# Layer 1 of a two-layer attention kernel: the output projection of a pair of rows as seven block products, with sums and residual on GpSimd

## Chip, cores and metric

The kernel runs on one core of a Trainium2 chip. The metric is the device time of one execution in microseconds, as the median of several runs. In the profile PE is the TensorE matrix engine, PEld its weight load, DVE VectorE, ACT ScalarE, POOL GpSimd and SP SyncE, which here only issues transfers.

## The reference, cut to what matters

The input x is 128 rows of 256 positions with 256 channels. Layer 0 (row attention with 8 heads and a bias from a second tensor) adds its output to x; nothing of it is touched here. Layer 1 normalizes x by groups, runs banded attention with 4 heads along the positions of each row, projects, and adds the result to x:

```python
qkv = x2 @ w_in.T + b_in                      # x2: 128 rows, 256 positions, 256 channels
q, k, v = split into 4 heads of 64
scores = q @ k.T / sqrt(64), kept where |i - j| <= 16
out = softmax(scores) @ v                     # back to 256 positions x 256 channels
y = out @ w_out.T + b_out
x = x + y
```

## The kernel before

Everything is float32. The output projection of one row is a 256x256 by 256x256 product; two rows are handled together, as a "pair", so layer 1 has 64 pairs. Its work is written in one hand-ordered loop (a manual schedule): each engine runs its instructions strictly in the order in which the Python calls issue them. An iteration p of the loop handles five pairs at different stages: `was` (pair p-1, whose second row is still to be applied and whose projection is due), `now` (p), `nxt` (p+1, whose q, k and v are being projected), `nn` (p+2, being centred) and `n3` (p+3, being loaded).

The steps that matter, by method:

- `scores(r)`: 32 small score matmuls of row r, an exp on ACT, and the band mask as a product with `bw` on POOL (L2020).
- `apply(r)`: the weighted values into the PSUM tiles `o_eo` (L2034), and the softmax sums into `su_eo` (L2042). `copy_sums`, `copy_odd` (ACT) and `join_sums`, `join_odd` (DVE) add the even and odd halves; `invert` is a reciprocal of 1.7 us on DVE (L2065), `weigh` the product of both on DVE (L2070), which gives `oT[r]`, the transposed attention output of the row. `weigh(1)` also issues a small store on SP.
- `product(n, i)` and `join(n, i)`: q, k and v (n = 0, 1, 2) of both rows of a pair as seven block products each, in Winograd's form of Strassen's scheme: 256x256 by 256x256 over a 2x2 grid, the two rows as one grid direction and the two halves of the channels as the other. Products accumulate in two PSUM banks x and y; ACT copies x out after products 1, 6 and 7, and after 4 to its place; DVE adds y and a copy after products 2, 5 and 3. For q and k a product is one matmul of 256 columns (L1956), for v two of 128 (L1952). The sums of weight blocks are made once (`mix_weights`), those of the input blocks by `differences` on POOL (L1918 to L1921).
- `turn` transposes the loaded pair on DVE (L1900), `centre(k)` normalizes one channel half on ACT (L1905), `add_bias` adds the output bias to the residual tile `xt` on POOL (L1911).
- `out_block(r, b)`: half the output projection of a row: two matmuls of 256 columns that accumulate over the two channel halves (L2088). They write `su_y[:, :, 1]`, half of a PSUM tile of two banks whose other half `su_y[:, :, 0]` holds the softmax sums (`su_eo`): bank 0 has `su_eo[0]` and the first block, bank 1 `su_eo[1]` and the second. `out_row` is two blocks and `keep_row`; `keep_row(r)` adds the residual on DVE (L2096), and after row 1 issues the store of the pair on SP.
- `some_checks(n)` pops small reductions and thresholds from a queue; they guard the fast path's assumptions. They are used up after some 28 pairs and come again in the last eight.

The order within an iteration before: scores of both rows; apply(1) of `was`; the products 1, 2, 6, 5, 7 of q and k with the joins of sums; join_odd, weigh and out_row(0) of `was`; products 4 and 3 of q and k; value products 1 and 2; apply(0) of `now`; then the value products 6, 5, 7, 4, 3 with the two out_blocks of row 1 among them, and at the end invert, weigh, the second centre, differences, add_bias and turn.

Of the kernel before, what the change touches and what calls it, by code (L numbers as in the profile page):

```python
# [16 lines left out]
P = 128  # L17
# [756 lines left out]
def fast_kernel(  # L774
# [134 lines left out]
    def rows(ap, s0, n):  # L909
        return ap[s0 : s0 + n].rearrange("s (b p) c -> p (s b) c", p=P)  # L910
# [333 lines left out]
    class Pair:  # L1244
# [251 lines left out]
        def keep_row(self, r):  # L1496
            s = 2 * self.p + r
            nc.vector.tensor_tensor(
                xo[:, (s % GB) * NB : (s % GB + 1) * NB, :], self.ps_y.rearrange("p (b c) -> p b c", b=NB),
                self.xt[:, r * NB : (r + 1) * NB, :], ALU.add,  # L1500
            )
            if (s + 1) % GB == 0:
                j = s // GB
                nc.sync.dma_start(
                    x1[j].rearrange("s (p b) c -> p s (b c)", b=NB), xo.rearrange("p (s b) c -> p s (b c)", b=NB)
                )
            n = GB if s < S - GB else GB // 2 if s < S - GB // 2 else GB // 4
            if (s + 1) % n == 0:
                at = s + 1 - n
                moments_of(xo[:, at % GB * NB : (at % GB + n) * NB, :], at, n)  # L1510
# [310 lines left out]
    with tc.tile_pool(name="l1", bufs=2) as sb, tc.tile_pool(  # L1821
# [10 lines left out]
        dev = lrs[0][:, :G]  # L1832
        each = head.rearrange("p n d -> p (n d)").rearrange("p (n c) -> p n c", n=2)
        wst = sb.tile([P, 4, 3, P], F32, name="wst", bufs=1)

        def norm1():

# [20 lines left out]
        def mix_weights():  # L1858

            a = [[w_in[:, k].rearrange("p (n m c) -> p m n c", n=3, m=KC)[:, m] for k in range(KC)]  # L1860
                 for m in range(KC)]
            s1, s2, s3, s4 = (wst[:, n] for n in range(4))
            nc.gpsimd.tensor_tensor(s1, a[1][0], a[1][1], ALU.add)
            nc.gpsimd.tensor_tensor(s2, s1, a[0][0], ALU.subtract)
            nc.gpsimd.tensor_tensor(s3, a[0][0], a[1][0], ALU.subtract)
            nc.gpsimd.tensor_tensor(s4, a[0][1], s2, ALU.subtract)
# [9 lines left out]
        class Pair1:  # L1876
# [55 lines left out]
            def product(self, n, i):  # L1932

                if len(self.ps) == n:
                    self.ps.append([mm1("ps_qk", n % 2) for _ in range(2)])
                    self.u.append(sm.tile([P, 3, I], F32, name="u1", tag=f"u{n}", bufs=2))
                x, y = (ps[:, :I] for ps in self.ps[n])
                w = lambda m, k: w_in[:, k, n * C + m * P : n * C + (m + 1) * P]
                b = lambda k, r: self.xgT[:, k, r * I : (r + 1) * I]
                to, lhs, rhs, start = {  # L1940
                    1: (x, w(0, 0), b(0, 0), True),
                    2: (y, w(0, 1), b(1, 0), True),
                    6: (x, wst[:, 1, n], self.dT[:, 1], False),
                    5: (y, wst[:, 0, n], self.dT[:, 0], True),
                    7: (x, wst[:, 2, n], self.dT[:, 2], False),
                    4: (x, w(1, 1), self.dT[:, 3], False),
                    3: (y, wst[:, 3, n], b(1, 1), False),
                }[i]
                if n == 2:
                    for b in range(NB):  # L1950
                        at = slice(b * P, (b + 1) * P)
                        nc.tensor.matmul(  # L1952
                            to[:, at], rhs[:, at], lhs, start=start and b == 0, stop=True, skip_group_check=True
                        )
                else:
                    nc.tensor.matmul(to, lhs, rhs, start=start, stop=True, skip_group_check=True)  # L1956
                u = self.u[n]
                if i in (2, 5, 3):
                    return
                at = (1, 6, 7, 4).index(i)  # L1960
                to = self.to[n](1, 0) if i == 4 else u[:, at]
                if n == 2:
                    nc.scalar.copy(to, x.rearrange("p (b c) -> p b c", b=NB) if i == 4 else x)
                else:
                    nc.scalar.activation(to, x, AF.Identity, bias=bin_c[:, n * KC + (at > 1) : n * KC + (at > 1) + 1])  # L1965
# [116 lines left out]
            def out_block(self, r, b):  # L2082
# [4 lines left out]
                for k in range(KC):  # L2087
# [2 lines left out]
                        start=(k == 0), stop=(k == KC - 1),  # L2090
                    )

            def keep_row(self, r):
                if r == 0:
                    self.yo = sb.tile([P, 2 * NB, C], F32, name="yo", tag="yo")
                nc.vector.tensor_tensor(  # L2096
                    self.yo[:, r * NB : (r + 1) * NB, :], self.y,
                    self.xt[:, r * NB : (r + 1) * NB, :], ALU.add,
                )
                s0 = 2 * self.p  # L2100
                if self.p == NP - 1:
                    nc.sync.dma_start(rows(out, s0 + r, 1), self.yo[:, r * NB : (r + 1) * NB, :])
                elif r == 1:
                    nc.sync.dma_start(rows(out, s0, 2), self.yo)
# [28 lines left out]
        def some_checks(n):  # L2133
            for _ in range(n):
                queue = late or checks
                if queue:
                    queue.pop(0)()
# [6 lines left out]
        with tc.manual_schedule():  # L2144
# [16 lines left out]
            look_all(eb.rearrange("p h b i -> p (h b i)"), math.exp(-20.0))  # L2161
            n_eb = cols[0]

            was = Nobody()
            for p in range(NP - 1):
                nn = pair1(p + 2) if p == 0 else n3
                n3 = pair1(p + 3)
                if p == 0:
                    nn.turn()
                if p == 1:  # L2170
                    mask_t = sb.tile([S, I], F32, name="mask_all", bufs=1)
                    nc.sync.dma_start(mask_t, mask)
                    look_all(mask_t, 1e-15)
                    n_mask = cols[0]
                    load_sums(rsum.rearrange("n q r c i -> (n q r c i)"), "sums0")
                if p == NP - LATE + 2:
                    load_sums(rsum1[: NP - LATE].rearrange("n q r i -> (n q r i)"), "sums1")

                now.scores(0)
                now.scores(1)  # L2180
                was.apply(1)
                nxt.begin_fast()
                was.copy_sums(1)
                nxt.product(0, 1)
                was.copy_odd(1)
                nxt.product(1, 1)
                was.join_sums(1)
                for n in range(2):
                    nxt.product(n, 2)
                    nxt.join(n, 2)  # L2190
                was.invert(1)
                some_checks(p > 0)
                for i in (6, 5, 7):
                    for n in range(2):
                        nxt.product(n, i)
                for n in range(2):
                    nxt.join(n, 5)
                was.join_odd(1)
                was.weigh(1)
                was.out_row(0)  # L2200
                for n in range(2):
                    nxt.product(n, 4)
                    nxt.product(n, 3)
                    nxt.join(n, 3)
                fast = p < NP - 2
                if fast:
                    nxt.product(2, 1)
                    nxt.product(2, 2)
                    nxt.join(2, 2)
                nn.centre(0)  # L2210
                some_checks(2 if p > NP - LATE else 0)

                now.apply(0)
                now.copy_sums(0)
                if fast:
                    nxt.product(2, 6)
                    nxt.product(2, 5)
                now.copy_odd(0)
                now.join_sums(0)
                was.out_block(1, 0)  # L2220
                if fast:
                    nxt.product(2, 7)
                now.join_odd(0)
                some_checks(2 if p > NP - LATE else p > 0)
                was.out_block(1, 1)
                if fast:
                    nxt.join(2, 5)
                was.keep_row(1)
                if fast:
                    nxt.product(2, 4)  # L2230
                    nxt.product(2, 3)
                    nxt.join(2, 3)
                now.invert(0)
                now.weigh(0)
                nn.centre(1)
                nn.differences()
                nn.add_bias()
                n3.turn()
                if p == NP // 2:
                    below(0, n_eb, math.exp(20.0))  # L2240
                    below(n_eb, n_mask, 1e15)
                was, now, nxt = now, nxt, nn

            now.scores(0)
            was.apply(1)
            was.copy_sums(1)
            was.copy_odd(1)
# [102 lines left out]
```

## Time and profile before

| | us |
|---|---|
| median of 3 runs | 3133.21 (3131.51 to 3134.19) |
| the profiled execution's own time | 3134.36 |
| its span in the profile | 3132.6 |
| one pair in layer 1 (2511.42 to 2528.80) | 17.38 |
| mean granted TensorE clock | 0.985 |

The span is the time from the first instruction of the program to the last; the execution's own time includes what lies around it. Layer 1 takes about the last third of the span. A row of the timeline gives the start, the length, engine, line, operation, output and inputs, shape and count of a run of equal instructions, and in brackets the idle time before it and what ended it. A row of a group by form gives busy time and mean nanoseconds of one, then the idle time of the engine before them.

### The profile page before, as it was taken

To read this page: it belongs to the slowest core of one execution; us is meant where nothing else is said; L and a number is where in the kernel's file an instruction comes from. 1 tells how busy PE (TensorE), PEld (TensorE's weight loads), DVE (VectorE), ACT (ScalarE), POOL (GpSimd) and SP (SyncE) were. 2 spreads that over 40 slices of the span, in tenths; PEclk is the share of its full clock that TensorE was granted. 3 is DMA by queue.
4 is the path that set the end of the run, shared out by engine and by line. 5 is a ranking of instruction groups with operands and counts; after the bars stand their busy time and mean duration, and the time that the engine had idled before them with its cause. 6 is when DMAs were issued, how large, how long until landed. Compare 5 with 4: busy or idle time off the path is not lost.

```text
span 3132.6 us, 80584 instructions
## 1 busy us (share of the span) xinstructions
PE 3017.0 (96%) x33630; PEld 2096.3 (67%) x33630; DVE 2398.1 (77%) x4007; ACT 1574.6 (50%) x2639; POOL 2271.3 (73%) x1635
## 2 busy tenths in 40 slices
PE   5589999999999999999999999899999999999998
PEld 3345555655555565555555655588888888888886
DVE  7986777777777777777777777588888877777788
ACT  3454444444444444444444444355555555555554
POOL 3469998988899889889998987455555555555553
PEclk9799999999999999999999999899999999999999
DMA  9952333323333332333333232544343444343431
GB/s 360 389 173 59 97 71 99 93 66 91 99 99 69 99 97 65 89 98 99 69 99 99 64 92 71 117 93 94 92 95 92 95 92 94 90 97 88 98 93 53
DMA packets 690951, 328.16 MB, mean 105 GB/s; under 512 B 538673, under 2 KB 639921, under 8 KB 689425
## 3 DMA queue, kind: packets, MB, share of 16 engines
q1 hardware_dynamic: 686176, 320.28, 39.9%
q8 instruction: 266, 4.36, 0.6%
q10 hardware_dynamic: 4400, 2.63, 0.3%
q14 instruction: 109, 0.88, 0.1%
HBM read 254.09 MB, written 68.75 MB: 103 GB/s over the span
## 4 chain that ended last, share of the span: by engine, by line
PE 90%; DMA 4%; DVE 3%; issue 1%; POOL 1%; ACT 1%; SPq 0%; POOLq 0%; ACTq 0%; DVEq 0%
PE ps_p L1364 22%; PE ps_qk L1956 12%; PE ps_sc L1401 9%; PE ps_ov L1436 7%; PE ps_su_y L2088 7%; PE ps_v L1382 7%; PE ps_qk L1952 7%; PE ps_y L1491 7%; PE ps_o L2034 4%; PE ps_su L1444 3%; PE ps_sc L2009 3%; PE ps_su_y L2042 2%; DMA xa<-in_x_dram 1%; DVE st L1199 1%; DMA zt<-in_z_dram 1%
## 5 line engine op out<-in xcount | busy, mean ns | idle before, releaser
L1425 POOL TENSOR_TENSOR eboth<-e 128x512 f32<-128x512 f32 x512 | 746.9, 1479 | 175.9 <-PE ps_su L1444 95.5
L1421 DVE TENSOR_TENSOR e<-ps_sc,eb 128x1024 f32<-128x1024 f32 x384 | 458.2, 1221 | 290.5 <-ACT ps_sc L1413 289.9
L1413 ACT ACTIVATE ps_sc<-ps_sc 128x1024 f32<-128x1024 f32 x384 | 375.4, 1007 | 439.4 <-PE ps_sc L1401 308.0
L1401 PE MATMUL ps_sc<-qT,kT 32*128 32x256 f32 x4096 | 296.1, 401 | 0.1
L1919 POOL TENSOR_TENSOR dT<-xgT,dT 128x256 f32<-128x256 f32 x63 | 46.1, 731 | 315.7 <-ACT xgT L1905 315.7
L2020 POOL TENSOR_TENSOR e<-e,bw 128x384 f32<-128x384 f32 x256 | 248.4, 1001 | 10.7 <-ACT e L2018 10.7
L1401 PEld LDWEIGHTS ps_sc<-qT,kT 32*128 32x128 f32 x4096 | 186.3, 184 | 103.6 <-issue 90.6
L2088 PE MATMUL ps_su_y<-w_out,oT 128*128 128x256 f32 x1008 | 254.5, 385 | 0.9 <-DVE sums L2059 0.9
L1491 PEld LDWEIGHTS ps_y<-wo,oT 128*128 128x128 f32 x1024 | 194.7, 190 | 83.9 <-issue 44.7
L1364 PE MATMUL ps_p<-xgT,wg 128*128 128x512 f32 x512 | 249.1, 609 | 1.6 <-ACT xgT L1333 1.6
L1364 PE MATMUL ps_p<-xnT,wq 128*128 128x512 f32 x512 | 247.5, 605 | 1.5 <-POOL xnT L1351 1.4
L1436 PE MATMUL ps_ov<-e,v 128*32 128x256 f32 x4096 | 248.2, 383 | 0.0
L1491 PE MATMUL ps_y<-wo,oT 128*128 128x256 f32 x1024 | 243.1, 381 | 3.5 <-POOL oT L1481 2.7
L1382 PE MATMUL ps_v<-wv,xnT 128*128 128x256 f32 x1024 | 242.2, 379 | 0.0
L1364 PE MATMUL ps_p<-xnT,wk 128*128 128x512 f32 x512 | 240.7, 592 | 0.0
L1382 PEld LDWEIGHTS ps_v<-wv,xnT 128*128 128x128 f32 x1024 | 194.9, 190 | 54.7 <-issue 31.5
L2065 DVE RECIPROCAL rv<-sums 128x256 f32<-128x256 f32 x128 | 223.1, 1743 | 0.0
L1965 ACT ACTIVATE u<-ps_qk,bin_c 128x256 f32<-128x256 f32 x378 | 174.7, 477 | 94.9 <-PE ps_qk L1956 94.9
L2088 PEld LDWEIGHTS ps_su_y<-w_out,oT 128*128 128x128 f32 x1008 | 181.8, 190 | 22.4 <-DVE sums L2059 1.3
L1436 PEld LDWEIGHTS ps_ov<-e,v 128*32 128x32 f32 x4096 | 120.2, 110 | 109.2 <-issue 42.5
L1364 PEld LDWEIGHTS ps_p<-xnT,wk 128*128 128x128 f32 x512 | 97.2, 190 | 122.8 <-issue 122.8
L1371 ACT ACTIVATE gT<-ps_p,bg_c 128x512 f32<-128x512 f32 x128 | 88.0, 687 | 179.5 <-PE ps_p L1364 179.5
(229 smaller groups left out, 6553.3 us busy)
## 6 DMA issues: line engine op xcount, KB each, us to landing
xa<-in_x_dram SPq DMA_DIRECT2D x8, 4096.0 KB
xt<-in_x_dram SPq DMA_DIRECT2D x64, 512.0 KB
x<-xo SPq DMA_DIRECT2D x16, 2048.0 KB
xt<-x SPq DMA_DIRECT2D x64, 512.0 KB
rvb<-rsum SPq DMA_DIRECT2D x252, 128.0 KB
xs<-x SPq DMA_DIRECT2D x252, 128.0 KB
out_dram<-yo SPq DMA_DIRECT2D x63, 512.0 KB
xs<-in_x_dram SPq DMA_DIRECT2D x248, 128.0 KB
```

The source lines that it names most:

```text
L1364: nc.tensor.matmul(ps, w[:, k, m * P : (m + 1) * P], getattr(self, src)[:, k, :], start=(k == 0), stop=(k == KC - 1),)
L1382: nc.tensor.matmul(self.ps_v[:, b * C : (b + 1) * C], self.xnT[:, k, t * P : (t + 1) * P], wv[:, k, :], start=(k == 0), stop=(k == KC - 1),)
L1401: nc.tensor.matmul(self.pss[q // 2][:, q % 2, b, :], self.kT[rs, c, r * I + b * P : r * I + (b + 1) * P], self.qT[rs, c, r * I : (r + 1) * I],
L1413: nc.scalar.activation(self.pss[a], ps, AF.Exp)
L1421: nc.vector.tensor_tensor(es[a], pss[a], eb[:, h : h + 2], ALU.mult)
L1425: nc.gpsimd.tensor_tensor(t, es[a][:, :, 0, :], es[a][:, :, 1, :], ALU.add)
L1436: nc.tensor.matmul(ov[q * D0 : (q + 1) * D0, c, :], self.v[:, r, b, h * D0 : (h + 1) * D0], es[q // 2][:, q % 2, b, :], start=(b == 0), st ...
L1491: nc.tensor.matmul(self.ps_y[:, b * C : (b + 1) * C], self.oT[r][:, k, b * P : (b + 1) * P], wo[:, k, :], start=(k == 0), stop=(k == KC - 1),)
L1956: nc.tensor.matmul(to, lhs, rhs, start=start, stop=True, skip_group_check=True)
L2020: nc.gpsimd.tensor_tensor(e[:, q], e[:, q], bcast(bw.rearrange("p b w -> p (b w)"), 1, KC), ALU.mult)
L2065: nc.vector.reciprocal(self.rv[:, r, :], self.sums)
L2088: nc.tensor.matmul(self.y[:, b], self.oT[r][:, k, b * P : (b + 1) * P], w_out[:, k, :], start=(k == 0), stop=(k == KC - 1),)
```

## The change

The two rows' output projection becomes seven block products over a 2x2 grid, like q, k and v. New are the sums of `w_out` blocks (`wso`), the sums of `oT` blocks on POOL (`row_sums`), the products (`out_product`), the joins on DVE (`out_join`) and the residual and store (`keep_rows`). `keep_rows` adds the residual on POOL for a pair one iteration later than before (`old`, pair p-2). `out_row(0)` and the two `out_block(1, b)` leave the loop's body; the order of the rest changes with them: join_odd(1) moves ahead, products 4 of q and k follow products 7 directly, product 3 of k goes among the value products, and both centres, differences, add_bias and turn move from the end of the iteration to before apply(0). The buffers of `u` go from two to one. The last two pairs, after the loop, are projected as before.

```diff
+        wso = sb.tile([P, 4, P], F32, name="wso", bufs=1)
...
+            a = [[w_out[:, k, m * P : (m + 1) * P] for k in range(KC)] for m in range(KC)]
+            s1, s2, s3, s4 = (wso[:, n] for n in range(4))
             nc.gpsimd.tensor_tensor(s1, a[1][0], a[1][1], ALU.add)
             nc.gpsimd.tensor_tensor(s2, s1, a[0][0], ALU.subtract)
             nc.gpsimd.tensor_tensor(s3, a[0][0], a[1][0], ALU.subtract)
...
-                    self.u.append(sm.tile([P, 3, I], F32, name="u1", tag=f"u{n}", bufs=2))
+                    self.u.append(sm.tile([P, 3, I], F32, name="u1", tag=f"u{n}", bufs=1))
...
+            def row_sums(self):
+
+                self.oS = sb.tile([P, 4, I], F32, name="oS1", tag="oS", bufs=1)
+                b = [[self.oT[r][:, k, :] for r in range(2)] for k in range(KC)]
+                t1, t2, t3, t4 = (self.oS[:, n] for n in range(4))
+                nc.gpsimd.tensor_tensor(t1, b[0][1], b[0][0], ALU.subtract)
+                nc.gpsimd.tensor_tensor(t2, b[1][1], t1, ALU.subtract)
+                nc.gpsimd.tensor_tensor(t3, b[1][1], b[0][1], ALU.subtract)
+                nc.gpsimd.tensor_tensor(t4, b[1][0], t2, ALU.subtract)
+
+            def quarter(self, m, r):
+                return self.yo[:, r * NB : (r + 1) * NB, m * P : (m + 1) * P]
+
+            def out_product(self, i):
+
+                if i == 1:
+                    self.yo = sb.tile([P, 2 * NB, C], F32, name="yo", tag="yo")
+                    self.uy = sm.tile([P, 3, I], F32, name="uy1", tag="uy", bufs=1)
+                x, y = (su_y[:, n, 1] for n in range(2))
+                w = lambda m, k: w_out[:, k, m * P : (m + 1) * P]
+                b = lambda k, r: self.oT[r][:, k, :]
+                to, rhs, lhs, start = {
+                    1: (x, w(0, 0), b(0, 0), True),
+                    2: (y, w(0, 1), b(1, 0), True),
+                    6: (x, wso[:, 1], self.oS[:, 1], False),
+                    5: (y, wso[:, 0], self.oS[:, 0], True),
+                    7: (x, wso[:, 2], self.oS[:, 2], False),
+                    4: (x, w(1, 1), self.oS[:, 3], False),
+                    3: (y, wso[:, 3], b(1, 1), False),
+                }[i]
+                for n in range(NB):
+                    at = slice(n * P, (n + 1) * P)
+                    nc.tensor.matmul(
+                        to[:, at], lhs[:, at], rhs, start=start and n == 0, stop=True, skip_group_check=True
+                    )
+                if i in (2, 5, 3):
+                    return
+                if i == 4:
+                    nc.scalar.copy(self.quarter(1, 0), x.rearrange("p (b c) -> p b c", b=NB))
+                else:
+                    nc.scalar.copy(self.uy[:, (1, 6, 7).index(i)], x)
+
+            def out_join(self, i):
+                m, r, at = {2: (0, 0, 0), 5: (1, 1, 2), 3: (0, 1, 1)}[i]
+                y, u = (t.rearrange("p (b c) -> p b c", b=NB) for t in (su_y[:, 1, 1], self.uy[:, at]))
+                nc.vector.tensor_tensor(self.quarter(m, r), y, u, ALU.add)
+
+            def keep_rows(self):
+                nc.gpsimd.tensor_tensor(self.yo, self.yo, self.xt, ALU.add)
+                nc.sync.dma_start(rows(out, 2 * self.p, 2), self.yo)
...
                 now.scores(0)
                 now.scores(1)
+                old.keep_rows()
                 was.apply(1)
...
                 was.join_sums(1)
+                was.join_odd(1)
                 for n in range(2):
                     nxt.product(n, 2)
                     nxt.join(n, 2)
                 was.invert(1)
-                some_checks(p > 0)
                 for i in (6, 5, 7):
                     for n in range(2):
                         nxt.product(n, i)
                 for n in range(2):
                     nxt.join(n, 5)
-                was.join_odd(1)
+                nxt.product(0, 4)
+                nxt.product(1, 4)
+                nxt.product(0, 3)
+                nxt.join(0, 3)
                 was.weigh(1)
-                was.out_row(0)
-                for n in range(2):
-                    nxt.product(n, 4)
-                    nxt.product(n, 3)
-                    nxt.join(n, 3)
+                nn.add_bias()
+                was.row_sums()
                 fast = p < NP - 2
                 if fast:
                     nxt.product(2, 1)
                     nxt.product(2, 2)
                     nxt.join(2, 2)
                 nn.centre(0)
-                some_checks(2 if p > NP - LATE else 0)
+                nn.centre(1)
+                nn.differences()
+                n3.turn()
 
                 now.apply(0)
                 now.copy_sums(0)
                 if fast:
                     nxt.product(2, 6)
                     nxt.product(2, 5)
+                now.join_sums(0)
+                was.out_product(1)
+                was.out_product(2)
+                was.out_join(2)
                 now.copy_odd(0)
-                now.join_sums(0)
-                was.out_block(1, 0)
+                now.join_odd(0)
                 if fast:
                     nxt.product(2, 7)
-                now.join_odd(0)
-                some_checks(2 if p > NP - LATE else p > 0)
-                was.out_block(1, 1)
-                if fast:
                     nxt.join(2, 5)
-                was.keep_row(1)
+                was.out_product(6)
+                was.out_product(5)
                 if fast:
                     nxt.product(2, 4)
+                some_checks(2 if p > NP - LATE else p > 0)
+                was.out_product(7)
+                was.out_join(5)
+                nxt.product(1, 3)
+                nxt.join(1, 3)
+                if fast:
                     nxt.product(2, 3)
                     nxt.join(2, 3)
+                was.out_product(4)
+                was.out_product(3)
+                was.out_join(3)
                 now.invert(0)
                 now.weigh(0)
-                nn.centre(1)
-                nn.differences()
-                nn.add_bias()
-                n3.turn()
+                some_checks(2 if p > NP - LATE else p > 0)
...
-                was, now, nxt = now, nxt, nn
+                old, was, now, nxt = was, now, nxt, nn
 
             now.scores(0)
+            old.keep_rows()
             was.apply(1)
```

More of the change, by code (lines that the diff above doesn't have):

```diff
@@ L1862, in mix_weights @@
             s1, s2, s3, s4 = (wst[:, n] for n in range(4))
+            nc.gpsimd.tensor_tensor(s1, a[1][0], a[1][1], ALU.add)
+            nc.gpsimd.tensor_tensor(s2, s1, a[0][0], ALU.subtract)
+            nc.gpsimd.tensor_tensor(s3, a[0][0], a[1][0], ALU.subtract)
+            nc.gpsimd.tensor_tensor(s4, a[0][1], s2, ALU.subtract)
+            a = [[w_out[:, k, m * P : (m + 1) * P] for k in range(KC)] for m in range(KC)]
+            s1, s2, s3, s4 = (wso[:, n] for n in range(4))
             nc.gpsimd.tensor_tensor(s1, a[1][0], a[1][1], ALU.add)
@@ L2162, in fast_kernel @@
             n_eb = cols[0]
-            was = Nobody()
+            old = was = Nobody()
             for p in range(NP - 1):
```

## The prediction, made before the run

> **What bounds the kernel now.** I read the page first, then the busy times of one pair's stretch, then the groups by form within layer 1, and last the timeline of that pair. In what follows T counts microseconds from a pair's first score matmul, which is 2511.42 in the pair shown. The page:
>
> ```profile
> span 3132.6 us, 80584 instructions
> PE 3017.0 (96%) x33630; PEld 2096.3 (67%) x33630; DVE 2398.1 (77%) x4007; ACT 1574.6 (50%) x2639; POOL 2271.3 (73%) x1635
> PE 90%; DMA 4%; DVE 3%; issue 1%; POOL 1%; ACT 1%; SPq 0%; POOLq 0%; ACTq 0%; DVEq 0%
> ```
>
> The chain that ended last is PE for 90%. One pair of layer 1, from score matmul to score matmul:
>
> ```profile
> 2511.42:2528.80 17.38, 17.38 (x297) 15.07 (x296) 13.37 (x20) 9.88 (x24) 9.50 (x9) 1.00 0.42 93
> ```
>
> PE has no gap in 17.38 us; DVE is busy 13.37, ACT 9.88, POOL 9.50. So a pair's length is PE's issue time plus whatever PE waits for. Unit costs (groups by form, layer 1):
>
> ```profile
> L2088 PE MATMUL ps_su_y<-w_out,oT 128*128 128x256 f32 x968 | 244.6, 385 | 0.0
> L1911 POOL TENSOR_TENSOR xt<-xt,bout_r 128x1024 f32<-128x1024 f32 x63 | 150.2, 2385 | 0.0
> L2096 DVE TENSOR_TENSOR yo<-ps_su_y,xt 128x512 f32<-128x512 f32 x121 | 82.9, 685 | 2.1
> L1963 ACT COPY u<-ps_qk 128x256 f32<-128x256 f32 x183 | 68.2, 373 | 100.8 <-PE ps_qk L1952 100.8
> L1918 POOL TENSOR_TENSOR dT<-xgT 128x256 f32<-128x256 f32 x62 | 45.3, 730 | 179.3 <-ACT xgT L1905 179.3
> ```
>
> A matmul's mean overlaps the next one, so PE is priced by the distance between starts (timeline; start, length; an f32 matmul shows as two records):
>
> ```profile
> 2516.02 2.75 PE L1956 MATMUL ps_qk<-dT,wst 128*128 128x256 f32 x12
> 2518.38 0.91 ACT L1965 ACTIVATE u<-ps_qk,bin_c 128x256 f32<-128x256 f32 x2 [0.82 <-PE ps_qk L1956]
> 2518.61 1.89 PE L2088 MATMUL ps_su_y<-w_out,oT 128*128 128x256 f32 x8
> 2518.89 0.42 DVE L1972 TENSOR_TENSOR qT<-ps_qk,u 128x256 f32<-128x256 f32 x1 [0.51 <-ACT u L1965]
> 2520.34 0.59 PE L1956 MATMUL ps_qk<-dT,w_in 128*128 128x256 f32 x2
> 2520.38 1.26 DVE L2070 TENSOR_TENSOR oT<-odd,rv 128x512 f32<-128x512 f32 x1
> 2524.55 1.16 PE L1952 MATMUL ps_qk<-wst,dT 128*128 128x128 f32 x8
> 2525.54 1.13 PE L2088 MATMUL ps_su_y<-w_out,oT 128*128 128x256 f32 x4
> 2527.82 0.61 PE L1952 MATMUL ps_qk<-w_in,dT 128*128 128x128 f32 x4
> 2528.26 0.61 PE L1952 MATMUL ps_qk<-wst,xgT 128*128 128x128 f32 x4
> ```
>
> Eight 256-column records take 2518.61 to 2520.34: 0.215 each. Four 128-column records take 2527.82 to 2528.26: 0.11 each. After a wait the first record costs 0.10 more, its weights not being loaded ahead: the eight from 2524.55 take 0.99, not 0.89. Two more stretches, for a lock and for a wait:
>
> ```profile
> 2304.49 0.74 POOL L1920 TENSOR_TENSOR dT<-xgT 128x256 f32<-128x256 f32 x1
> 2304.85 0.93 DVE L2070 TENSOR_TENSOR oT<-odd,rv 128x512 f32<-128x512 f32 x1
> 2305.18 1.19 POOL L1921 TENSOR_TENSOR dT<-xgT,dT 128x256 f32<-128x256 f32 x1
> ...
> 3100.07 0.42 DVE L2059 TENSOR_TENSOR sums<-ps_su_y,sums 128x256 f32<-128x256 f32 x1 [0.29 <-ACT sums L2053]
> 3100.55 0.51 PEld L2088 LDWEIGHTS ps_su_y<-w_out,oT 128*128 128x128 f32 x3 [1.30 <-DVE sums L2059]
> ```
>
> **What the Trainium skill says.** "SBUF — State Buffer", Who interferes with whom: a DVE instruction with two SBUF inputs and a GpSimd instruction that reads SBUF exclude each other for a whole instruction. The trace agrees: weigh (L2070, both inputs SBUF, 0.69 alone) that arrives in L1920 takes 0.93, and the next POOL add takes 1.19 instead of 0.73; at 2520.38, in a mask product on POOL, weigh takes 1.26. DVE gets in after the current POOL instruction, not after the queue. "PSUM — Partial Sum Buffer", PSUM bank collisions: engines must be kept apart by bank, not by address. The trace agrees: at 3100.55 the output projection waited 1.30 for join_sums, which reads other columns of the same bank. "Perfetto Trace Analysis", Optimizing Scalar/DVE Operations: moving work between DVE and GpSimd might not help because of the shared port.
>
> **The change, part by part.**
>
> *PE work.* Removed: the 16 records of L2088, 1.73 + 0.97 (2525.54 to 2526.51) + 0.87 = 3.57. Added: 7 products of 4 records, 28 x 0.111 = 3.12. Gain 0.45 a pair. All else on PE only moves.
>
> *New waits of PE*, in its order:
> (a) Product 5 of q needs join(0,2) off its bank. Now join(0,2) ends at T 4.86 and product 5 starts at 5.46. join_odd(1) goes ahead of it: its copy ends at T 4.46, plus 0.68, plus 0.42, with hand-over 5.6. So 0.14 and a restart 0.10: +0.24.
> (b) Product 4 of q adds to the bank that the copy of product 7 reads. That copy ends at about 2518.85 (the join behind it starts at 2518.89), and the last product 7 is issued by 2518.61. Now out_row(0) lies between (1.73 us); afterwards nothing does. 0.28 + 0.10 = +0.38.
> (c) Value product 2 needs join(0,3)'s buffer. Now about 0.21 is lost there. Afterwards join(0,3) follows its product at once: 0.42 to read it and 0.42 to add, against 0.445 of product 1 in between and the rest of product 3's issue: 0.23 + 0.10. +0.12.
> (d) The first output product waits for join_sums(0) (same bank). On DVE now stand weigh(1), join(2,2), the transpose (1.24, moved here from T 2.84) and join_sums(0). On POOL: the mask products can start at T 1.5 (first exp); weigh(0) arrives at T 2.2, waits to 2.4 and holds POOL for 0.6; four of 0.97 end at 5.85; keep_rows, priced as L1911, at 8.2; add_bias at 10.55. weigh(1) arrives at 9.7 after join(0,3), in the middle of add_bias, and gets in at 10.4: ends 11.1. join(2,2) 11.45, transpose 12.65, join_sums 13.0. PE, with (a) to (c), arrives at 12.68; it starts at 13.02 plus restart. +0.44.
>
> From there to the pair's end 4.99 of PE work follow (ten products of 0.445, one of 0.43, a change of tile shape 0.1). I checked each wait in it: copies of x (0.31 to read, 0.37) have at least one other product as cover; out_join(5) ends near 17.3 against 17.6 when product 3 needs it; join(1,3) near 17.7 against the next scores at 18.1. Nothing added.
>
> *Costed at nothing.* ACT gets four copies of 0.37, 1.5 us, to 11.4 of 17.4; centre(1) moves to before apply(0) and ends about when the sums are ready (cost if late: 0.1). DVE loses two adds of 0.685 and gets three joins of 0.42. row_sums (4 x 0.73 from L1918, up to 1.2 when held) start at 11.1 and yield the second by 12.7; output product 6 needs it at 14.5: hidden by 1.8. differences then end near 17, before the next mask product at T 1.5 of the next pair. POOL totals 9.5 + 2.4 + 2.9 + holds 1.2 = 16. keep_rows has no row of its own: 2.36 as L1911, at most 2.9 if it is held; each 0.1 lengthens (d). The x loads are queued on SP behind the weigh store (T 11) rather than the output store (T 17.3): 6 earlier, for a transpose 9 earlier; some 13 us remain after the last issue (15 now), so 0, with 0 to 0.5 as bounds. The output store waits on SP for keep_rows, to T 8; behind it only the weigh store. Four more weight sums at the start (2.9) lie in POOL's idle 4.4.
>
> *Sum.* -0.45 + 0.24 + 0.38 + 0.12 + 0.44 = +0.73: a pair of 18.1. 61 full pairs: +45. In some 27 pairs a check's threshold instruction stands after weigh(0) and waits for POOL too: (a) grows by 0.4, of which (d) swallows some: 0.3 x 27 = +8. The last pair in the loop without value products, two checks after weigh in the last six pairs and a longer drain: +5. Together +58 on a span of 3132.6: 3190.6. The profiled run's time (3134.36) is 1.8 above its span, and the median of the runs (3133.21) 1.2 below that: 3191.
>
> **Rivals.**
> 1. Only PE's waits (a) to (c): POOL is earlier than I think or the first product isn't held. For: PE arrives only 0.34 before join_sums. Against: the wait at 3100.55. +0.29 x 61 + 4: 3155.
> 2. Faster: DVE is never late. Place: the DVE queue at join_odd(1) and weigh(1); then (a), (c) and (d) are gone and the old loss of 0.21 with them; (b), an ACT latency, stays: -0.45 - 0.21 + 0.38 = -0.28, 3117. It decides if DVE runs 0.15 earlier at join(0,2) and 0.4 earlier at join_sums(0). For: DVE is busy 13.4 of 17.4. Against: copy_odd's end is set by PE and ACT.
> 3. The two banks are guarded as one tile: every output product then waits 0.73 for the read before it, less 0.445: seven times about 0.35 with a restart, +2.5 more a pair, 3340. For: it is one tile. Against: now the second block waits for nothing of the first.
> 4. The waits and the gain cancel: 3133.
>
> **How the numbers follow.** Mine 0.52, rival 1 0.24, rival 2 0.15, rival 4 0.05, rival 3 0.04. My own case spans 3165 to 3235 (keep_rows up to 2.9 is +33; (d) half as large is -13). The range of 3135 to 3235 takes in rival 1 and the upper part of rival 4 and leaves out rivals 2 and 3. 0.2% (6.3 us) is what a measurement can tell from no change. Faster 0.15, same 0.05, slower 0.80.
>
> **What would show it.** Right: pairs of 18.1; PE waiting for ACT u before L1956's product 4; L2070 of row 1 longer than 1 us with the bias add on POOL; the first output product waiting for DVE sums. Wrong: pairs under 17.4 with no PE gap (rival 2), or an output product waiting for the copy of the one just before it (rival 3).

## The result and the profile after

| | us |
|---|---|
| before, median of 4 runs | 3132.6 (3131.51 to 3134.19) |
| after, median of 4 runs | 3369.67 (3368.79 to 3370.18) |
| ratio | 1.0752, 95% interval 1.074 to 1.0765 |
| spans of the two profiles | 3132.6 and 3367.8 |

The kernel became 7.5% slower, against 1.9% predicted, and the range ended at 3235. From the page after, the lines that were shown of before:

```profile
PE 3115.3 (93%) x34374; PEld 2113.1 (63%) x34374; DVE 2396.2 (71%) x4069; ACT 1663.7 (49%) x2887; POOL 2585.9 (77%) x1949
PE 79%; DVE 8%; ACT 4%; DMA 4%; issue 3%; POOL 2%; SPq 0%; ACTq 0%; DVEq 0%; POOLq 0%
```

PE's share of the chain fell from 90% to 79%, and DVE's and ACT's rose from 3% and 1% to 8% and 4%. The time is in layer 1: PE no longer fills it. Busy times of one pair after (stretch, its length, then PE, PEld, DVE, ACT, POOL, clock and transfers):

```profile
2600.00:2621.00 21.00, 18.83 (x307) 14.88 (x306) 12.67 (x21) 10.88 (x26) 14.56 (x15) 1.00 0.33 77
```

A pair takes 21.0 us instead of 17.38, and PE is idle for over 2 us of it; no other engine is full. The mean distance between first score matmuls over 59 pairs rose from 17.44 to 21.14 us: 3.70 more, times 61 is 226 of the 235 us between the spans. What PE waits for, in the view of waits (total, times, longest, window 2200 to 3200):

```profile
PE ps_su_y L2132 <- ACT uy L2140: 43.8, 95, 0.5
PE ps_su_y L2132 <- ACT yo L2138: 24.0, 47, 0.8
PE ps_su_y L2132 <- DVE yo L2145: 10.6, 47, 0.6
PE ps_qk L1963 <- ACT u L1972: 10.3, 46, 0.2
```

The first three are the new output products (L2132) waiting for the copies and joins that read them. The window holds 47 pairs, so 95 waits for `uy` are two a pair. The timeline of the output products of one pair shows which:

```profile
2630.41 0.71 PE L2132 MATMUL ps_su_y<-w_out,oT 128*128 128x128 f32 x4
...
2631.15 0.37 ACT L2140 COPY uy<-ps_su_y 128x256 f32<-128x256 f32 x1 [0.62 <-PE ps_su_y L2132]
...
2631.57 0.71 PE L2132 MATMUL ps_su_y<-w_out,oT 128*128 128x128 f32 x4 [0.46 <-ACT uy L2140]
...
2632.12 0.61 PE L1959 MATMUL ps_qk<-wst,dT 128*128 128x128 f32 x4
...
2632.95 0.68 PE L2132 MATMUL ps_su_y<-wso,oS 128*128 128x128 f32 x4 [0.22 <-DVE yo L2145]
...
2634.10 0.71 PE L2132 MATMUL ps_su_y<-wso,oS 128*128 128x128 f32 x4 [0.46 <-ACT uy L2140]
...
2635.97 0.61 PE L1959 MATMUL ps_qk<-wst,xgT 128*128 128x128 f32 x4
2636.71 0.68 PE L2132 MATMUL ps_su_y<-w_out,oS 128*128 128x128 f32 x4
...
2637.90 0.71 PE L2132 MATMUL ps_su_y<-wso,oT 128*128 128x128 f32 x4 [0.51 <-ACT yo L2138]
```

Read the second product, which writes bank y: it starts at 2631.57, when ACT has copied the first one out (2631.15 + 0.37). It needs nothing of that copy, which reads bank x. A product of four records takes 0.445; from the start of one to the start of the next it is here 1.16 (2630.41 to 2631.57). So product 2 waits 0.71. In the same way product 6 waits 0.38 for the join that reads y, though it writes x; product 5 waits 0.70 for the copy of x, though it writes y; product 4 waits 0.29 for the second join of y, though it writes x; product 3 waits 0.74 for the last copy of x. With three restarts of 0.10 (the first record after a wait) that is 3.1 us a pair, about as much as was lost beyond the forecast (21.0 less 18.1). An output product that waits for the copy of the one just before it is the sign that the prediction had named for its rival 3. The idle times in brackets are smaller than these, since a matmul's shown length reaches past its issue time.

### The profile page after: what moved, and what is told of

Same layout as the page of the kernel before. It is cut to its first block, busy times and chain, and to the rows that moved or that the text cites. A ratio compares the mean times of both kernels' runs of the same rounds, so it can differ in the third digit from the quotient of the medians.

```text
span 3367.8 us, 83103 instructions
## 1 busy us (share of the span) xinstructions
PE 3115.3 (93%) x34374; PEld 2113.1 (63%) x34374; DVE 2396.2 (71%) x4069; ACT 1663.7 (49%) x2887; POOL 2585.9 (77%) x1949
## 4 chain that ended last, share of the span: by engine, by line
PE 79%; DVE 8%; ACT 4%; DMA 4%; issue 3%; POOL 2%; SPq 0%; ACTq 0%; DVEq 0%; POOLq 0%
PE ps_p L1364 20%; PE ps_qk L1963 9%; PE ps_sc L1401 8%; PE ps_su_y L2132 8%; PE ps_ov L1436 7%; PE ps_v L1382 6%; PE ps_y L1491 6%; PE ps_qk L1959 5%; PE ps_su L1444 3%; PE ps_o L2041 2%; PE ps_sc L2016 2%; DMA xa<-in_x_dram 1%; ACT uy L2140 1%; DMA zt<-in_z_dram 1%; DVE rv L2072 1%
## 5 line engine op out<-in xcount | busy, mean ns | idle before, releaser
L2027 POOL TENSOR_TENSOR e<-e,bw 128x384 f32<-128x384 f32 x256 | 278.1, 1116 | 360.7 <-ACT e L2025 360.7
L2145 DVE TENSOR_TENSOR yo<-ps_su_y,uy 128x256 f32<-128x256 f32 x186 | 79.0, 425 | 353.4 <-PE ps_su_y L2132 158.0
L1963 PE MATMUL ps_qk<-dT,wst 128*128 128x256 f32 x756 | 187.8, 388 | 7.0 <-DVE qT L1979 7.0
L1116 POOL TENSOR_TENSOR zrs<-zrs,mhalf 128x32 f32<-128x32 f32 (+1 forms) x19 | 88.0, 4634 | 114.1 <-DVE zrs L1109 114.0
```

The source lines that it names most:

```text
L2027: nc.gpsimd.tensor_tensor(e[:, q], e[:, q], bcast(bw.rearrange("p b w -> p (b w)"), 1, KC), ALU.mult)
```

## The experiments

Theory G: the PSUM tile `su_y` spans two banks, and the program guards it as one: a write to either bank waits until the last read of either bank is done. This is the prediction's third rival. Theory P: the time went to GpSimd, which got about 5 us of work more a pair (14.56 busy where it was 9.50), and to the port that it shares with VectorE.

| run | median us | ratio to before (95%) | length of an undisturbed pair |
|---|---|---|---|
| kernel before | 3132.6 | 1 | 17.38 |
| changed kernel | 3369.67 | 1.0752 (1.074 to 1.0765) | 21.0 |
| e1_two_tiles | 3185.82 | 1.017 (1.0153 to 1.0187) | 17.96 |
| e2_before_two_tiles | 3137.04 | 1.0012 (1.0003 to 1.002) | 17.44 |
| e3_no_residual | 3367.26 | 1.0745 (1.0727 to 1.0763) | 20.9 |
| e4_two_tiles_reordered | 3096.9 | 0.9886 (0.987 to 0.9903) | 16.74 |
| e5_two_tiles_odd_later | 3175.7 | 1.0136 (1.0119 to 1.0153) | 17.96 |
| e6_two_tiles_sums_first | 3181.35 | 1.0155 (1.0138 to 1.0172) | 17.9 |
| e7_one_tile_reordered | 3240.39 | 1.0341 (1.0324 to 1.0359) | 18.9 |

The pair's length is the median distance of first score matmuls over the later pairs, in which no checks are left.

### e1: two tiles of one bank each

```diff
-        su_y = ps_o.tile([P, 2, 2, I], F32, name="ps_su_y1", tag="su")
-        su_eo = [su_y[:, n, 0] for n in range(2)]
+        su_y = [ps_o.tile([P, 2, I], F32, name=f"ps_su_y1_{n}", tag=f"su{n}") for n in range(2)]
+        su_eo = [su_y[n][:, 0] for n in range(2)]
...
-                x, y = (su_y[:, n, 1] for n in range(2))
+                x, y = (su_y[n][:, 1] for n in range(2))
```

The other uses of `su_y` follow; the loop issues the same instructions in the same order.

> The changed kernel with the PSUM tile of sums and projection made as two tiles of one bank each; the same instructions in the loop, so output products that write bank 0 need not wait for a read of bank 1. Theory G (the two banks are guarded as one tile, and every output product waits for the copy or join of the one before it): the pair falls from 21.0 to between 17.7 and 18.1 us and the time to 3155 to 3195. Theory P (the time went to GpSimd: sums, residual and the port shared with VectorE): stays at 3350 to 3370, since GpSimd's work is the same.

3185.82: 184 of the 237 us came back, 3.0 a pair, with GpSimd's work unchanged (14.59 us busy in a pair). Theory P falls, G holds. The program itself shows the reason. The waits that it attaches to the output products, in the changed kernel and in e1 (from the list of PE's instructions; the suffix is the tile, Activation is ACT and Pool is POOL, whose waits are for the row sums):

```
changed kernel                            e1
product 1  su_y   waits DVE               su_y_0  waits DVE
product 2  su_y   waits Activation        su_y_1  waits Activation
product 6  su_y   waits DVE, Pool         su_y_0  waits Activation, Pool
product 5  su_y   waits Activation        su_y_1  waits DVE
product 7  su_y   waits Pool              su_y_0  waits Activation, Pool
product 4  su_y   waits DVE, Pool         su_y_0  waits Activation, Pool
product 3  su_y   waits Activation        su_y_1  waits DVE
```

In e1 products 6, 7 and 4 wait for the copy of x and 5 and 3 for the join of y: the true needs. Products 1 and 2 wait for `join_sums` and `copy_sums`, which read other columns of the same tile. In the changed kernel a product waits for whichever read came last, of x or y (product 7 for none: nothing reads the tile between the read that product 5 waited for and product 7). The timeline of e1 at the same place:

```profile
2615.24 1.16 PE L2134 MATMUL ps_su_y<-w_out,oT 128*128 128x128 f32 x8
...
2616.23 0.61 PE L1960 MATMUL ps_qk<-wst,dT 128*128 128x128 f32 x4
...
2616.68 1.06 PE L2134 MATMUL ps_su_y<-wso,oS 128*128 128x128 f32 x8
```

Products 1 and 2 run as eight records in a row, 0.99 to the next start; products 6 and 5 likewise, 0.89.

### e2: the kernel before with two tiles

> The kernel before with the same split into two tiles (its residual add becomes two adds of 256 columns, VectorE 4 x 0.42 instead of 2 x 0.685 us a pair). Theory G: in the old order the second block waited for nothing of the first and the first waits for join_sums of its own bank, so no gain: 3125 to 3145. If the split itself frees something also in the old order: below 3120.

3137.04, within the first case and 0.1% above the kernel before. The old order had no read between writes of the two banks, so the guard cost it nothing, and splitting the tile is no gain by itself. The pair is 0.06 longer; VectorE's residual add is two instructions there.

### e3: without the residual add on GpSimd

```diff
-                nc.gpsimd.tensor_tensor(self.yo, self.yo, self.xt, ALU.add)
```

> The changed kernel without the residual add on GpSimd (2.35 us a pair); the output lacks x of layer 0's result and the output bias. Theory G: GpSimd is not what PE waits for, 3360 to 3372. Theory P: 2 us and more a pair come back, 3240 or less.

3367.26 against 3369.67. The stretch of a pair, columns as above:

```profile
2600.00:2620.90 20.90, 18.86 (x308) 15.09 (x307) 12.33 (x21) 10.92 (x27) 12.28 (x14) 1.00 0.36 77
```

POOL has 2.3 us less to do, and the pair stays at 20.9. GpSimd was not what PE waited for.

### e5 and e6: single terms of the remainder

After e1, 53 us stay above the kernel before. e5 moves one line:

```diff
-                was.join_odd(1)
                 for n in range(2):
                     nxt.product(n, 2)
                     nxt.join(n, 2)
+                was.join_odd(1)
```

> e1_two_tiles with only join_odd(1) put back behind the joins of product 2. Theory: term (a), 0.24 us a pair, goes, so 14 us: 3168 to 3176. Rival: the next wait, for the copy of product 7 or for join_sums, takes it over: 3180 to 3188.

3175.7 lies in the theory's span, but the trace shows the rival at work. In pairs without checks nothing was gained: 17.96 in both kernels. One such pair of e5:

```profile
2784.57 2.75 PE L1964 MATMUL ps_qk<-dT,wst 128*128 128x256 f32 x12
...
2791.56 1.16 PE L1960 MATMUL ps_qk<-wst,dT 128*128 128x128 f32 x8
...
2792.79 1.16 PE L2134 MATMUL ps_su_y<-w_out,oT 128*128 128x128 f32 x8
```

The twelve records take 2.75 again instead of e1's 2.96, so (a) is gone. But PE comes that much earlier to the wait for join_sums: from the eight value records before it to the first output product it takes 1.23 here, where e1 has 1.11 (2614.13 to 2615.24). The medians over 29 later pairs say the same: 0.20 saved on q and k, 0.17 lost again before the first output product (1.09 to 1.26). PE's waits in the window 2200 to 3100 of e5 name join_sums 19 times (3.6 us), and e1's list does not. In the profiled executions e5's pairs are 8.3 us shorter in all: 5.1 in the first 28 and 1.6 in the last five, which have checks and in which (a) was larger, and 1.4 in the 29 between. So (a) by itself was worth nothing where no check stands, and it was luck that the time fell where the theory had it.

e6 only exchanges two lines of GpSimd's queue:

```diff
-                nn.add_bias()
                 was.row_sums()
+                nn.add_bias()
```

> e1_two_tiles with only the row sums ahead of the bias add on GpSimd, so that weigh(1) finds no bias add under way. If the port lock there delays PE (term (d)): up to 0.1 us a pair, 3177 to 3183. If PE's arrival at the first output product covers the delay: no change, 3183 to 3189.

3181.35 lies in the first case's span, but its interval overlaps e1's, so the times alone show no gain. The trace does, where no check stands: the median from the value records to the first output product falls from 1.09 to 0.99, which is the records and a restart with no wait left, and the pair from 17.96 to 17.9. With checks it is 0.99 in both, and nothing is gained. So it costs little here that GpSimd holds weigh up, though it does. The group of weigh, in e1 and then in e6:

```profile
L2078 DVE TENSOR_TENSOR oT<-odd,rv 128x512 f32<-128x512 f32 x110 | 107.9, 981 | 1.9
```

```profile
L2078 DVE TENSOR_TENSOR oT<-odd,rv 128x512 f32<-128x512 f32 x110 | 83.6, 760 | 1.9
```

Two of them a pair, 0.22 shorter each: 0.44 us of VectorE's time a pair vanished, and 0.06 of it reached the end of a pair without checks.

### e4: two tiles and another order

The order of e4 puts work of PE between each read and the write that waits for it. The lines shown leave out the old places of the calls that it moves, the moves of copy_odd, join_odd, the centres and differences to places among the output products, and that of join_odd(1), which is e5's:

```diff
                 for i in (6, 5, 7):
                     for n in range(2):
                         nxt.product(n, i)
+                now.apply(0)
+                now.copy_sums(0)
                 for n in range(2):
                     nxt.join(n, 5)
+                was.weigh(1)
+                was.row_sums()
+                nn.add_bias()
+                now.join_sums(0)
                 nxt.product(0, 4)
-                nxt.product(1, 4)
                 nxt.product(0, 3)
                 nxt.join(0, 3)
-                was.weigh(1)
+                nxt.product(1, 4)
...
+                was.out_product(1)
+                was.out_product(2)
...
                     nxt.product(2, 6)
                     nxt.product(2, 5)
+                now.invert(0)
...
                 if fast:
+                    nxt.product(2, 4)
+                was.out_product(4)
+                if fast:
                     nxt.product(2, 3)
                     nxt.join(2, 3)
-                was.out_product(4)
                 was.out_product(3)
                 was.out_join(3)
-                now.invert(0)
                 now.weigh(0)
+                n3.turn()
```

> Two tiles as in e1_two_tiles, and another order: apply(0) of the current pair moved between products 7 and 4 of q and k, product 3 of q ahead of product 4 of k, join_odd(1) behind the joins of product 2, the row sums ahead of the bias add on GpSimd, invert(0) among the output products, the transpose at the pair's end. If the terms (a), (b), (c) and (d) of the prediction are what keeps e1 at 18 us a pair, they go: 16.7 to 16.9 us a pair, 3090 to 3105, faster than both kernels. If seven products of 128 columns cost PE more than eight blocks of 256 whatever the order: 3133 or more.

3096.9: 1.1% faster than the kernel before, and 8% faster than the changed one. A pair:

```profile
2500.00:2516.75 16.75, 16.75 (x309) 14.80 (x309) 12.58 (x22) 11.11 (x27) 14.13 (x14) 1.00 0.41 98
```

PE is busy 16.75 of 16.75, and its waits from 2200 to 3000 hold a single entry of 0.7 us. The pair is the old one less the gain of PE's work and the old loss before value product 2: 17.38 - 0.45 - 0.21 = 16.72. So the seven products are worth what the issue times say, once nothing is waited for. e4 moves many things at once; what each move is worth was not measured.

### e7: the new order with one tile

> The order of e4_two_tiles_reordered with the one PSUM tile of two banks as in the changed kernel. The guard of the whole tile should still cost some 3 us a pair, as between the changed kernel and e1: 3270 to 3310. If the order alone were the matter: under 3130.

3240.39: 143 us above e4, with the same order but one tile, so the guard costs 2.2 us a pair (18.9 - 16.74) here, not 3, and the expected 3270 was too high. The waits of e7, window 2200 to 3100:

```profile
PE ps_su_y L2132 <- ACT uy L2140: 44.1, 95, 0.7
PE ps_su_y L2132 <- DVE yo L2145: 5.5, 16, 0.3
PE ps_su_y L2132 <- ACT yo L2138: 0.3, 1, 0.3
```

In e4's order a value product stands between the last copy of x and product 3, which covers most of that wait. The two for `uy` stay, with products 1 and 2 and products 6 and 5 side by side: in a pair of e7 products 2 and 5 lose 0.64 each, product 4 loses 0.29, product 3 loses 0.22, and four restarts add 0.4.

The four kernels make a square. The second tile is worth 184 us in the changed kernel's order and 143 in e4's; e4's order is worth 129 with one tile and 89 with two. Neither alone gets below the kernel before.

## Why the prediction was wrong

**The step that failed** is the last one of the waits: "I checked each wait in it ... Nothing added", on the 4.99 us after the first output product. It put at nothing what measured 3.0 us a pair (e1 to the changed kernel): five of the seven output products waited for reads of the other bank. The reason is rival 3, that the two banks are guarded as one tile, which got a chance of 0.04. I argued against it with "now the second block waits for nothing of the first". That was no evidence: in the old order nothing reads the first block before the second is written, so a guard of the tile and a guard of the bank look alike there (e2). The other observation that I leaned on, the wait at 3100.55 for join_sums, fits both as well: it shows that the guard is wider than the columns, not that it stops at the bank. (Its 1.30 us is the idle time of the weight load; the matmul itself stood for 0.92.) And the section "PSUM bank collisions raise a hardware error" of the Trainium skill's page "PSUM — Partial Sum Buffer" says that accesses of different engines to one bank and quadrant must be kept apart; it says nothing of the waits that a program gets for a tile of two banks. No run here tests that need itself: what the trace shows are the program's waits. I took the need for the wait.

The size of rival 3 was fair, though low: 2.5 more a pair, as seven waits of about 0.35, for 3.0. It took a product of 0.445 off every wait. That fits products 6 and 4, which have other products between the read and the write (0.38 and 0.29); products 2, 5 and 3 have none and wait 0.70 to 0.74. Products 1 and 7 had no wait of this kind.

**The rest of the sum** came out near once e1 took the guard away: 3185.8 against 3191, and the mean pair 18.16 against 17.44, +0.72, where +0.73 was forecast without the checks. Term by term, from e1's timeline:

```profile
2606.96 2.96 PE L1964 MATMUL ps_qk<-dT,wst 128*128 128x256 f32 x12
...
2610.15 1.10 PE L1964 MATMUL ps_qk<-dT,w_in 128*128 128x256 f32 x4 [0.23 <-ACT u L1973]
...
2611.52 1.39 PE L1960 MATMUL ps_qk<-w_in,xgT 128*128 128x128 f32 x8
...
2612.84 0.95 PE L2042 MATMUL ps_o<-e,v 64*32 64x96 f32 x61
...
2614.13 1.16 PE L1960 MATMUL ps_qk<-wst,dT 128*128 128x128 f32 x8
...
2614.80 0.38 DVE L2067 TENSOR_TENSOR sums<-ps_su_y,sums 128x256 f32<-128x256 f32 x1
```

- PE's gain of 0.45: right, by e4's 16.75. In e4's timeline the 28 records take 3.1 us, for 3.57 of the 16 before.
- (a) +0.24: the twelve records last 2.96 instead of 2.75, so 0.21. Undoing it alone gave nothing in a pair without checks, since (d) grew by as much (e5): the two are not independent terms of a sum.
- (b) +0.38: twelve records of 0.215 and (a) end at 2609.75; product 4 starts at 2610.15, 0.40, and the six records up to 2611.52 take 0.08 more than 1.29. 0.48: the hand-over from ACT to PE was sized too small.
- (c) +0.12: 2611.52 to 2612.84 is 1.32, where it was 1.19. 0.13.
- (d) +0.44: twice too large. The eight value records of 2614.13 and a restart end at 2615.12. join_sums ended at 2615.18 and the first product started at 2615.24: a wait of 0.12, and a restart of 0.10, since its eight records take 0.99 to the next start. 0.22. PE came 0.07 later than forecast and VectorE 0.2 earlier, and a term that is the difference of two such times took both errors. (The forecast of the mask products, 1.5 and four of 0.97 and 0.6, adds up to 5.98 and not to its 5.85; the trace has 5.84.) weigh(1) did meet the bias add, 1.33 us at 2612.06, as foretold.

The sum of these is +0.59, 17.97 for 17.96 measured. The first 28 pairs, with checks, take 18.12, so checks cost 0.16, not 0.3. (d) and the checks were sized too large and (b) too small, and some pairs are longer for reasons outside the sum (the 29 later pairs of e1 have a median of 17.97 and a mean of 18.10). That these partly cancel is why 3185.8 came so near to 3191: partly luck.

**Costed at nothing**, and rightly: GpSimd's added work (e3), ACT's copies (11.3 of 17.96 busy in e1), the earlier transpose and the queue of loads (no wait for a transfer is in PE's list).

The version that beats both kernels is e4. What isn't settled: what makes some of the later pairs longer, and what each move of e4 is worth. In e1 a product still waits for reads of other columns of its tile, so within that tile of one bank the guard is no finer; two tiles in one bank were not tried.

## What to carry to other kernels

In these kernels the program made the waits by tile, wider than the data needed: before a chain of short writes and reads goes into a shared PSUM tile, ask which tile each wait would name, and give each bank whose reads and writes alternate its own tile. An old order that never alternated says nothing about this. And count the work of PE between a read and the write that waits for it: a copy of 256 columns out of PSUM takes about 0.73 us here from the start of the last record to the next start on PE (0.31 until ACT starts, 0.37 for the copy and 0.05 after it). One product of 0.445 us in between left 0.22 uncovered in e7; with two, as between products 6 and 7 in e1, nothing was lost. And terms of such a sum are not independent: a wait that is taken away can come back at the next one (e5).

## What the runs showed of the hardware that I had not expected

Nothing new of the hardware caused the result. One thing was smaller than it looked: the port that GpSimd and VectorE share lengthened weigh by 0.22 us on average, 0.44 a pair, and at most 0.1 of it reached PE (e6).
